# A DRAM intermediate laid out by partition of a unit instead of by lines of eight columns

## The chip, the cores and the metric

The kernel runs on one core of one Trainium2 chip. The metric is the device time of one execution in microseconds (us). A measurement of a kernel is the median of several executions. Beside it stands one execution that the hardware profiler recorded; from it come the views of the profile.

## The reference: what is computed

The input x has 32 images of 48 channels, 64 rows and 128 columns, all float32. Two layers of the same form follow one another. Each normalises x in 16 groups of channels (per image), sends the result through four recurrent scans, and adds the outcome to x. A step of a scan is a 5-tap convolution over the line before it, plus a bias, plus the line's own input:

```python
def step(w, b):
    def f(carry, inp):
        nxt = inp + _conv1d(carry, w, b)
        return (nxt, nxt)
    return f
...
x = x + _L0_conv_ref(_gn(x), ...)   # rows down, rows up, columns right, columns left
x = x + _L1_conv_ref(_gn(x), ...)   # the same with layer 1's weights
```

Down and up go over the 64 rows (the convolution runs along the columns). Right and left go over the 128 columns (the convolution runs along the rows). No line can begin before the one before it is done.

## The kernel before

**Tiling.** The 32 images are four groups of eight (`GB = 8`). Eight columns (in the row scans) or eight rows (in the column scans), each with 48 channels, make 384 values, which fill three tiles of 128 partitions (`NG = 3`, the index `o`). The table `PIECES` says which partitions hold which channels of which of the eight. A step of a scan is nine matrix products into PSUM and three vector operations (line 929) that add bias and input and write the new line in place.

**Stages.** `PHASES` is worked off in order: for layer 0 the rows of groups 0 to 3 (down and up), then the columns of the pairs (0, 1) and (2, 3) (right and left); then the same for layer 1. The profile names the products of a stage by layer and group or pair: `step_10d` is layer 1, group 0, rows down, `step_10u` the same up, `step_01l` layer 0, pair 1, columns left. In layer 1 the stages of groups 2 and 3 are joined (`JOINED`): while one group goes up, the next goes down in the same products. These steps bear two names, `step_12u7d...` for row 7 up of group 2 beside row 56 down of group 3.

**The intermediate.** The result of layer 0 goes to four DRAM tensors `mid`, one for each group of images. It is written unit by unit. A unit is one tile `o` of one group of images over a quarter of the columns: 128 partitions with 8 KB each, 1 MB in all. `keep_result` (line 852) writes it, and `by_unit` (line 269) says where it lies. Layer 1 reads it twice:

- `take_rows` (line 766) loads rows for the row scans. For these a run of DRAM bytes is short: one row, one quarter of the columns, one channel of one of the eight columns, 128 bytes for 8 images and 4 values. `by_quarter` (line 263) gives the pattern. One call takes rows `h0` to `h1` of one tile `o`, and issues a DMA for each piece of `PIECES` and each of the four quarters. Over the three tiles that is 10 pieces times 4 quarters, 40 DMAs.
- `load_residual` (line 832) loads a unit for the addition after the column scans of layer 1, with DMAs that ScalarE's queue issues.

After `take_rows` has landed, `scale_rows` (line 783, instructions on line 790) normalises the rows in place on ScalarE, 24 activations a call, eight for each `o`. Then the scan may use the rows.

**The order of the work.** Everything beside the scans is put on an agenda by the unit of scan at which it should happen, and recorded between the scan's steps. On each engine, and on each queue, the instructions of the agenda stay in that order. Nearly all DMAs are issued by one queue, SyncE's (line 298). For layer 1, `plan_rows` asks for 16 rows at a time in the stages of groups 0 and 1, and for 8 rows at a time in the joined stages of groups 2 and 3:

```python
if k in JOINED:
    for i in range(H // E8):
        h, t = i * E8, t0 + 2 * i * E8
        for o in range(NG):
            at(t - 34 + 2 * o, take_rows, k, h, h + E8, o)
        at(t - 17, scale_rows, k, h, h + E8)
elif k:
    for i in range(4):
        if PHASES[k][1]:
            for o in range(NG):
                t = t0 + ahead[i] - 2 + 3 * o
                at(t, take_rows, k, i * LOAD, (i + 1) * LOAD, o)
```

Between the loads the same queue writes the rows that come out of the up scans (`upa`, `upb`), and, around the beginning of layer 1, loads residuals for layer 0 (`xin`) and writes the last units of `mid`.

Of the kernel before, what the change touches and what calls it, by code (L numbers as in the profile page):

```python
# [29 lines left out]
F32 = mybir.dt.float32  # L30
# [3 lines left out]
C = 48  # L34
# [8 lines left out]
E8 = 8  # L43
FULL = 128
NG = E8 * C // FULL
NQ = 4
# [75 lines left out]
def kernel(  # L122
# [8 lines left out]
    nc = tc.nc  # L131
    B, _, H, W = x.shape
    NK = W // E8
    NH = H // E8
# [4 lines left out]
    LINE = E8 * RUN  # L139
# [15 lines left out]
    dram = ctx.enter_context(tc.tile_pool(name="dram", bufs=1, space=bass.MemoryType.DRAM))  # L155
# [35 lines left out]
    def kept(name):  # L191
# [11 lines left out]
            for g in range(NGRP)  # L203
        ],
        [
            dram.tile([NQ, NH, E8 * C, LINE], F32, tag=f"mid{g}", name=f"mid{g}")
            for g in range(NGRP)
        ],
    ]
# [35 lines left out]
    def x_by_col(t, e, j):  # L245


        return t[e * NQ + j]
# [10 lines left out]
    def natural_col(t, e, j):  # L259

        return t.rearrange("c (a i) q n -> i q c a n", i=E8)[e, j]

    def by_quarter(t, e, h0, h1, q):


        t = t[q].rearrange("a (i c) (e n) -> e c (a i) n", i=E8, e=E8)
        return t[e, :, h0:h1]

    def by_unit(t, o, j):


        at = [(o * FULL, 0, FULL)]
        if o == NG - 1:
            at = [(6 * C, 0, 2 * C), (5 * C + C // 3, 2 * C, FULL)]
        t = t[j].rearrange("a m n -> m a n")
        return [(t[r : r + p1 - p0], p0, p1) for r, p0, p1 in at]

    def by_line(t):

        return t.rearrange("p (a n) -> p a n", a=NH)  # L280
# [16 lines left out]
    def dma(dst, src, queue=None):  # L297
        (queue or nc.sync).dma_start(dst, src)
# [21 lines left out]
    def pieces(o):  # L320
        return [(e, c0, c1, p0) for e, c0, c1, g, p0 in PIECES if g == o]
# [3 lines left out]
    def slots(k):  # L325

        return (0, 1, 2) if k % 2 == 0 else (2, 1, 0)
# [398 lines left out]
    def place(k, h):  # L726


        first = k
        while first in JOINED:  # L730
            first -= 1
        since = k - first
        turned = (since + 1) // 2 % 2 if h < HALF else since % 2
        c = h % HALF // E8
        return HALF // E8 - 1 - c if turned else c

    def rows_at(k, h0, h1):

        places = sorted(place(k, h) for h in range(h0, h1, E8))
        at = places[0] * E8 + h0 % E8  # L740
        assert h0 // HALF == (h1 - 1) // HALF and places[-1] - places[0] == len(places) - 1
        return row_views(k)[h0 // HALF][:, :, at : at + h1 - h0]
# [23 lines left out]
    def take_rows(k, h0, h1, o):  # L766

        _, layer, g = PHASES[k]
        turned = h1 - h0 > E8 and place(k, h0) > place(k, h0 + E8)
        if turned:  # L770
            for h in range(h0, h1, E8):
                take_rows(k, h, h + E8, o)
            return
        view = rows_at(k, h0, h1)
        for e, c0, c1, p0 in pieces(o):
            here = view[p0 : p0 + c1 - c0, o]
            for q in range(NQ):
                dma(
                    here[:, :, q * RUN : (q + 1) * RUN],
                    by_quarter(source[layer][g], e, h0, h1, q)[c0:c1],  # L780
                )
# [24 lines left out]
    def quarter(k, j):  # L806
        return slot[slots(k)[j % 3]].rearrange("p (o s n) -> p s o n", s=2, o=NG)
# [24 lines left out]
    def load_residual(k, j, i, nat):  # L832
        _, layer, pair = PHASES[k]
        o, half = UNITS[i]
        t = source[layer][2 * pair + half]
        if layer:
            for there, p0, p1 in by_unit(t, o, j):
                dma(by_line(nat)[p0:p1], there, nc.scalar)
        else:
            for e, c0, c1, p0 in pieces(o):  # L840
                here = nat[p0 : p0 + c1 - c0]
                if pair or half:
                    dma(here, x_by_col(t, e, j)[c0:c1])
                else:
                    dma(by_line(here), natural_col(t, e, j)[c0:c1])
# [6 lines left out]
    def keep_result(k, j, i):  # L852
        _, layer, pair = PHASES[k]
        o, half = UNITS[i]
        for there, p0, p1 in by_unit(source[1][2 * pair + half], o, j):
            dma(there, by_line(quarter(k, j)[:, half, o])[p0:p1])

    def by_image(t):

# [210 lines left out]
    def plan_rows(k, t0, prev):  # L1070
# [11 lines left out]
# [12 lines that stand above are left out]
                else:  # L1094
                    at(t0 + ahead[i], move_rows, k, i * LOAD, (i + 1) * LOAD, False)
                at(t0 + scaled[i], scale_rows, k, i * LOAD, (i + 1) * LOAD)
# [19 lines left out]
    def plan_cols(k, t0, prev):  # L1116
# [32 lines left out]
        for u, (t, j, i) in enumerate(direct):  # L1149
            nat = tiles[u % n]  # L1150
            o, half = UNITS[i]
            if u < n:
                at(left + 16, load_residual, k, j, i, nat)
            if layer == 0:
                if u >= n:
                    at(max(direct[u - n][0] + 3, t - 21), load_residual, k, j, i, nat)
                at(t, add_residual, k, j, i, nat)
                at(t + 4, keep_result, k, j, i)
                unit = quarter(k, j)[:, half, o]
                if half == 0:  # L1160
                    for b in range(GB):
                        at(t + 5 + b, stats[0].take, j, o, unit, b)
                else:
                    at(t + 1, stats[1].take, j, o, unit)
            else:

                at(t, add_residual, k, j, i, nat)
                at(t + 2.5, permute_unit, k, j, i, nat, (nc.gpsimd, nc.scalar, nc.scalar))
                if final or j not in HELD:
                    at(t + 4.5, store_result, k, j, i, nat)  # L1170
                else:
                    at(t + 4.5, hold_result, j, i, nat)
                if final and j == 1:
                    at(t + 4.7, load_residual, k, 0, i, last_tiles(k)[i])

                if u >= 2 and u - 2 + n < len(direct):
                    at(t + 4.6, load_residual, k, *direct[u - 2 + n][1:], tiles[(u - 2) % n])
# [27 lines left out]
    for k, (kind, *_) in enumerate(PHASES):  # L1205
        n = (H if kind == "rows" else W) - 1
# [283 lines left out]
```

## Time and profile before

| what | us |
|---|---|
| median of 3 runs | 4110.29 (4107.43 to 4110.69) |
| profiled execution, its own time | 4108.49 |
| its span, first to last instruction | 4106.8 |
| TensorE (PE) busy | 4012.3 |
| VectorE (DVE) busy | 2078.8 |
| ScalarE (ACT) busy | 1306.9 |
| GpSimd (POOL) busy | 789.0 |

The span is what the profile shows; 1.7 us of the execution lie outside it. Mean granted clock of TensorE is 0.991 of full speed. SyncE (SP) only issues DMAs, so it has no busy time in this table; its issues stand in the timeline under SPq, as start, duration, what is written and read, and how many. ScalarE's queue stands under ACTq.

### The profile page before, as it was taken

The numbers are of one execution on the slowest core, as the hardware profiler recorded it, in microseconds if no ns is written. First come the engines' busy times: TensorE is split into PE (matmuls) and PEld (weight loads), VectorE is DVE, ScalarE is ACT, GpSimd is POOL, SyncE is SP. The second block draws the span as 40 slices with busy tenths as digits, with TensorE's granted clock in tenths as the row PEclk, the third lists the DMA queues.
The fourth block names the chain that finished last, engine by engine and source line by source line (L and its number), as shares of the span: only waits on it lengthen the run. The fifth ranks groups of instructions, "written<-read, shape, count | busy, mean of one in ns | idle before, by whom it ended". The sixth has DMA issues, their size and how long they took to land. (4 is left out here: it accounts for less than half of the span.)

```text
span 4106.8 us, 85201 instructions
## 1 busy us (share of the span) xinstructions
PE 4012.3 (98%) x34360; PEld 3927.0 (96%) x34360; DVE 2078.8 (51%) x6137; ACT 1306.9 (32%) x2628; POOL 789.0 (19%) x672
## 2 busy tenths in 40 slices
PE   6999999999999999999999999999999999999994
PEld 5999999999999999999999998888999999999994
DVE  6454454544444567546655443333444444444444
ACT  4557466430000355003773633434000002300122
POOL 5631303100000243002411000000000025610353
PEclk9999999999999999999999999999999999999997
DMA  9898897967993499804996965666698039999799
GB/s 299 220 223 185 245 189 218 171 108 97 147 181 60 141 245 288 193 2 155 242 161 143 142 102 96 101 108 104 103 166 202 1 77 245 299 251 155 147 234 196
DMA packets 2253898, 681.57 MB, mean 166 GB/s; under 512 B 2008848, under 2 KB 2206656, under 8 KB 2231232
## 3 DMA queue, kind: packets, MB, share of 16 engines
q1 hardware_dynamic: 2117568, 595.36, 70.3%
q10 hardware_dynamic: 135936, 80.77, 8.2%
q8 instruction: 270, 4.42, 0.5%
q14 instruction: 124, 1.02, 0.1%
HBM read 399.11 MB, written 295.93 MB: 169 GB/s over the span
## 5 line engine op out<-in xcount | busy, mean ns | idle before, releaser
L850 POOL TENSOR_TENSOR arena<-arena 128x2048 f32<-128x2048 f32 x80 | 362.5, 4547 | 1714.3 <-PE step_00l L915 521.3
L790 ACT ACTIVATE arena<-arena,offsetr,scaler 128x128 f32<-128x128 f32 (+1 forms) x576 | 345.2, 688 | 348.8 <-DMA arena<-mid 322.5
L648 ACT ACTIVATE early<-arena 128x256 f32<-128x256 f32 x192 | 129.7, 676 | 837.0 <-POOL arena L850 830.6
L790 ACT ACTIVATE arena<-arena,offset,scale 128x256 f32<-128x256 f32 (+2 forms) x360 | 249.0, 787 | 91.8 <-DMA arena<-xin 81.6
L709 POOL COPY arena<-arena 128x256 f32<-128x256 f32 x340 | 201.0, 653 | 383.7 <-DMA arena<-in_x 230.2
L915 PE MATMUL step_01r<-arena,early 128*128 128x128 f32 x2286 | 249.8, 272 | 0.0
L915 PE MATMUL step_11r<-arena,early 128*128 128x128 f32 x2286 | 249.2, 272 | 0.0
L915 PEld LDWEIGHTS step_11r<-arena,early 128*128 128x128 f32 x2286 | 248.7, 184 | 0.4 <-DVE arena L929 0.3
L915 PEld LDWEIGHTS step_01r<-arena,early 128*128 128x128 f32 x2286 | 248.9, 184 | 0.2
L915 PE MATMUL step_00r<-arena,early 128*128 128x128 f32 x2286 | 248.8, 272 | 0.0
L915 PEld LDWEIGHTS step_00r<-arena,early 128*128 128x128 f32 x2286 | 248.5, 184 | 0.2 <-DVE arena L929 0.2
L915 PE MATMUL step_10l<-arena,wleft 128*128 128x128 f32 x2286 | 248.5, 272 | 0.0
L915 PE MATMUL step_11l<-arena,wleft 128*128 128x128 f32 x2286 | 248.5, 272 | 0.0
L915 PE MATMUL step_00l<-arena,wleft 128*128 128x128 f32 x2286 | 248.4, 272 | 0.0
L915 PE MATMUL step_01l<-arena,wleft 128*128 128x128 f32 x2286 | 248.4, 272 | 0.0
L915 PE MATMUL step_10r<-arena,early 128*128 128x128 f32 x2286 | 248.4, 272 | 0.0
L915 PEld LDWEIGHTS step_10l<-arena,wleft 128*128 128x128 f32 x2286 | 248.4, 184 | 0.0
L915 PEld LDWEIGHTS step_11l<-arena,wleft 128*128 128x128 f32 x2286 | 248.4, 184 | 0.0
L915 PEld LDWEIGHTS step_00l<-arena,wleft 128*128 128x128 f32 x2286 | 248.4, 184 | 0.0
L915 PEld LDWEIGHTS step_01l<-arena,wleft 128*128 128x128 f32 x2286 | 248.4, 184 | 0.0
L915 PEld LDWEIGHTS step_10r<-arena,early 128*128 128x128 f32 x2286 | 248.4, 184 | 0.0
L872 ACT COPY arena<-arena 128x256 f32<-128x256 f32 x172 | 99.6, 656 | 366.6 <-POOL arena L850 234.7
(545 smaller groups left out, 6870.1 us busy)
## 6 DMA issues: line engine op xcount, KB each, us to landing
xin<-arena SPq DMA_DIRECT2D x94, 512.0 KB, 4.5
arena<-in_x SPq DMA_DIRECT2D x18, 2048.0 KB, 10.5
upa<-arena SPq DMA_DIRECT2D x192, 192.0 KB, 3.8
arena<-upa SPq DMA_DIRECT2D x96, 384.0 KB, 9.9
arena<-xin SPq DMA_DIRECT2D x96, 384.0 KB, 10.6
upb<-arena SPq DMA_DIRECT2D x192, 192.0 KB, 3.9
arena<-upb SPq DMA_DIRECT2D x96, 384.0 KB, 10.9
arena<-xin SPq DMA_DIRECT2D x174, 192.0 KB, 4.2
```

What stands on the lines that cost most here:

```text
L648: nc.scalar.activation(junk[:, 0:n], view[:, b], AF.Identity, accum_out=self.sum[:, i, j : j + 1])
L709: copy(dst[:, r, q], src[:, r0 + r, q])
L790: nc.scalar.activation(args[0], args[0], AF.Identity, bias=args[2], scale=args[1])
L850: eng.tensor_tensor(unit, unit, nat, ALU.add)
L872: copy(by_w(perm)[:, a], src[:, a])
L915: nc.tensor.matmul(part(turn(whole(ps[o]))[0:m], -s), weights[:, i, at : at + m], part(turn(src(i)), s), start=seen[o] == 1, stop=seen[o] ...
```

## The change

The DRAM tensors `mid` change from [quarter, row block of 8, 384, 256] to [quarter, 384, 2048]. A partition of a unit, which lay in eight runs of 1 KB, now lies in one run of 8 KB. The same bytes are written and read.

For `keep_result` and `load_residual` the access becomes plain, 128 partitions by 2048 elements. For `take_rows` the row index now lies in two dimensions of DRAM, the block of eight rows and the row within it, with different strides, where it was one dimension before. So 16 rows are no longer one pattern: the function calls itself for each 8 rows. Before, it did so only for places that run backwards.

```diff
-            dram.tile([NQ, NH, E8 * C, LINE], F32, tag=f"mid{g}", name=f"mid{g}")
+            dram.tile([NQ, E8 * C, NH * LINE], F32, tag=f"mid{g}", name=f"mid{g}")
...
     def by_quarter(t, e, h0, h1, q):
-        t = t[q].rearrange("a (i c) (e n) -> e c (a i) n", i=E8, e=E8)
-        return t[e, :, h0:h1]
+        t = t[q].rearrange("(i c) (a e n) -> e a c i n", i=E8, a=NH, e=E8)
+        return t[e, h0 // E8, :, h0 % E8 : h0 % E8 + h1 - h0]
...
     def by_unit(t, o, j):
         at = [(o * FULL, 0, FULL)]
         if o == NG - 1:
             at = [(6 * C, 0, 2 * C), (5 * C + C // 3, 2 * C, FULL)]
-        t = t[j].rearrange("a m n -> m a n")
-        return [(t[r : r + p1 - p0], p0, p1) for r, p0, p1 in at]
+        return [(t[j, r : r + p1 - p0], p0, p1) for r, p0, p1 in at]
...
     def take_rows(k, h0, h1, o):
-        turned = h1 - h0 > E8 and place(k, h0) > place(k, h0 + E8)
-        if turned:
+        if h1 - h0 > E8:
             for h in range(h0, h1, E8):
                 take_rows(k, h, h + E8, o)
             return
...
-                dma(by_line(nat)[p0:p1], there, nc.scalar)
+                dma(nat[p0:p1], there, nc.scalar)
...
-            dma(there, by_line(quarter(k, j)[:, half, o])[p0:p1])
+            dma(there, quarter(k, j)[p0:p1, half, o])
```

In the instructions, the change is on two queues. The first place is SyncE's queue where it first loads rows for layer 1, behind the last units of `mid` of a column quarter (shapes are partitions, rows and elements; `mid_84` is group 0's intermediate). Before:

```order
L298 DMA mid_87<-arena 96x8x256
L298 DMA mid_87<-arena 32x8x256
L298 DMA arena<-mid_84 48x16x32 x8
L298 DMA arena<-mid_84 32x16x32 x4
L298 DMA arena<-mid_84 16x16x32 x4
L298 DMA arena<-mid_84 48x16x32 x8
L298 DMA arena<-mid_84 16x16x32 x4
L298 DMA arena<-xin_82 48x2048 x2
```

And with the change (its line numbers are one lower from here on):

```order
L297 DMA mid_87<-arena 96x2048
L297 DMA mid_87<-arena 32x2048
L297 DMA arena<-mid_84 48x8x32 x8
L297 DMA arena<-mid_84 32x8x32 x4
L297 DMA arena<-mid_84 48x8x32 x8
L297 DMA arena<-mid_84 32x8x32 x4
L297 DMA arena<-mid_84 16x8x32 x4
L297 DMA arena<-mid_84 48x8x32 x8
L297 DMA arena<-mid_84 16x8x32 x8
L297 DMA arena<-mid_84 48x8x32 x8
L297 DMA arena<-mid_84 16x8x32 x4
L297 DMA arena<-xin_82 48x2048 x2
```

The 28 loads of 16 rows have become 56 loads of 8 rows, and the load from `xin` behind them stands 28 places later on the queue.

The second place is ScalarE's queue, where it loads the first residuals of layer 1. Before:

```order
L298 DMA arena<-mid_84 128x8x256
L298 DMA arena<-mid_85 128x8x256
L298 DMA early<-mid_84 96x8x256
L298 DMA early<-mid_84 32x8x256
L872 COPY arena<-arena 128x256 x15
```

And with the change:

```order
L297 DMA arena<-mid_84 128x2048
L297 DMA arena<-mid_85 128x2048
L297 DMA early<-mid_84 96x2048
L297 DMA early<-mid_84 32x2048
L870 COPY arena<-arena 128x256 x15
```

Their number and order stay; only the shape is another. TensorE, VectorE and GpSimd have the same instructions in the same order in both kernels.

## Prediction, on record before the result

> **What bounds the kernel now.** I read first the busy times, then the span in three stretches, then who issues the loads, then how early they land.
>
> ```profile
> PE 4012.3 (98%) x34360; PEld 3927.0 (96%) x34360; DVE 2078.8 (51%) x6137; ACT 1306.9 (32%) x2628; POOL 789.0 (19%) x672
> ...
> 82.30:4050.30 3968.00, 3964.95 (x34139) 3891.95 (x34137) 1999.81 (x6014) 1252.83 (x2526) 731.21 (x566) 1.00 0.78 162
> 4050.30:4106.80 56.50, 0.00 (x0) 0.00 (x0) 24.82 (x19) 13.31 (x23) 12.73 (x18) 0.51 1.30 170
> ```
>
> The second and third rows are stretches of the span (length, then PE, PEld, DVE, ACT and POOL busy, clock, DMA share, GB/s). From 82 to 4050 us PE is busy 3964.95 of 3968.00 us: the chain of scan steps runs without a pause. Then come 56.5 us of final stores. The edit touches no step, so between 82 and 4050 it can gain next to nothing; it can lose, if rows come late. Whether they do is decided on SyncE's queue, here where layer 1 begins (start, duration, what, how many):
>
> ```profile
> 1998.71 22.81 SPq L298 DMA_DIRECT2D arena<-mid  x28
> ...
> 2023.52 12.87 SPq L298 DMA_DIRECT2D arena<-mid  x12
> ...
> 2039.35 16.31 SPq L298 DMA_DIRECT2D arena<-mid  x12
> ...
> 2056.29 18.83 SPq L298 DMA_DIRECT2D arena<-mid  x28
> ...
> 2080.42 18.69 SPq L298 DMA_DIRECT2D arena<-mid  x28
> ...
> 2101.37 10.21 SPq L298 DMA_DIRECT2D arena<-mid  x12
> ...
> 2114.11 10.09 SPq L298 DMA_DIRECT2D arena<-mid  x12
> ...
> 2126.22 21.29 SPq L298 DMA_DIRECT2D arena<-mid  x28
> ...
> 2212.65 50.96 SPq L298 DMA_DIRECT2D arena<-mid  x80
> 2263.71 39.70 SPq L298 DMA_DIRECT2D upb<-arena  x40
> 2303.50 50.79 SPq L298 DMA_DIRECT2D arena<-mid  x80
> 2354.39 19.89 SPq L298 DMA_DIRECT2D upb<-arena  x20
> ```
>
> Group 0's 160 loads take 131.10 us together (the first eight rows), group 1's 101.75 (two rows). 2212.65 + 50.96 + 39.70 + 50.79 ends at 2354.3, where the next row begins: the queue has no free time. It goes on so through the joined stages:
>
> ```profile
> 2505.00 8.99 SPq L298 DMA_DIRECT2D upb<-arena  x10
> 2514.04 21.34 SPq L298 DMA_DIRECT2D arena<-mid  x40
> 2535.52 9.03 SPq L298 DMA_DIRECT2D upb<-arena  x10
> 2544.59 15.42 SPq L298 DMA_DIRECT2D arena<-mid  x28
> ...
> L915 PE MATMUL step_12u15d<-arena,early x18: 366/379/379, 2869.9 to 2873.5; 128*128 128x256 f32 x12, 128*96 128x240 f32 x4, 128*112 128x256 f32 x2
> L915 PE MATMUL step_12u7d<-arena,early x18: 366/379/379, 2900.5 to 2904.2; 128*128 128x256 f32 x12, 128*96 128x240 f32 x4, 128*112 128x256 f32 x2
> ```
>
> One round of 40 loads and 10 writes goes from 2514.04 to 2544.59, 30.55 us, and the eight double steps that use it take 2900.5 − 2869.9 = 30.6 us. So queue and PE are level there: a delay that the queue has when the joined stages begin is still there at their end. What is to spare shows between the end of the scaling (ACT) and the first product that needs the rows:
>
> ```profile
> ACT arena L790 <- DMA arena<-mid: 322.5, 49, 21.2
> ...
> 2149.28 6.06 ACT L790 ACTIVATE arena<-arena,offsetr,scaler 128x256 f32<-128x256 f32 x8 [0.54 <-DMA arena<-mid]
> 2870.81 4.18 ACT L790 ACTIVATE arena<-arena,offsetr,scaler 128x128 f32<-128x128 f32 x8 [3.27 <-DMA arena<-mid]
> ...
> L915 PE MATMUL step_10d<-arena,early x1134: 266/275/377, 2070.3 to 2195.7; 128*128 128x128 f32 x126, 128*96 128x120 f32 x63
> ```
>
> The scaling waits for the loads 49 times: it ends when they let it. Group 0's last 16 rows are scaled at 2149.28 + 6.06 = 2155.3. The 63 steps from 2070.3 to about 2196 take 1.99 us each at most, so row 48 is begun some 47 steps after 2070.3, at 2163: 8 us to spare. The last rows of the joined stages are ready at 2870.81 + 4.18 = 2875.0 and needed at 2900.5: 25.5 us to spare.
>
> **The change part by part.** *More issues.* Groups 0 and 1 had 320 loads of 16 rows; they become 640 of 8 rows. The joined stages already use 8 rows, so the price of the new form stands in the profile: 21.34 us for 40, 0.534 us each. A group now takes 320 × 0.534 = 170.7 us of the queue.
>
> - Group 1: 170.7 − 101.75 = **+69.0 us**.
> - Group 0: 170.7 − 131.10 = **+39.6 us** at least. Its present loads are slower than group 1's by 131.10 − 101.75 = 29.35 us, since they stand between large transfers. If all of that stays, it is +69.0 us. Smaller DMAs leave the transfer engines more room to clear the large ones meanwhile, but the queue still has to wait where a large one fills it; I take the middle, **+54.3**.
>
> Together +123.3 us, with bounds of 108.6 and 138.0. The room that I speak of stands in this stretch of the joined loads (DMA share before the last number):
>
> ```profile
> 2514.00:2535.40 21.40, 21.40 (x102) 18.36 (x101) 7.62 (x17) 8.37 (x16) 0.00 (x0) 1.00 0.54 85
> ```
>
> The 16 engines are used for 0.54 of it, so the queue's issuing, not the data, sets the 0.534 us. The Trainium skill, "DMA: Bandwidth & Descriptors", section "Rules for kernel authors", says to join small transfers, since below 64 KB a transfer is mostly overhead; the change splits 96 KB into 48 KB, and the share of 0.54 agrees.
>
> *What hides it.* PE can wait only once for a delay of the queue: by the end of the joined stages it has lost the largest excess of delay over what was to spare. The delay is the full 123.3 from the end of group 1's loads on, and the least to spare after that is 25.5. So PE stands 123.3 − 25.5 = **97.8 us** later (83.1 to 112.5). The first part falls in group 0's down scan: 54.3 − 8 = 46 us by row 48. Behind these loads on the queue stand `xin` loads, `upb` writes and the joined loads; they shift with it, and what shifts no more than PE costs nothing more.
>
> *Clock.* After a pause PE starts slower:
>
> ```profile
> 76.50 7.72 PE L915 MATMUL step_00d<-arena,early 128*128 128x128 f32 x43 [4.07 <-DVE arena L929]
> 80.00:120.00 40.00, 39.25 (x348) 39.05 (x346) 18.18 (x57) 15.99 (x36) 24.51 (x16) 0.97 0.79 125
> ```
>
> 43 products took 7.72 us where 348 later ones took 39.25 (4.85 for 43): 2.9 us lost after a pause of 4.07. Between two late loads this only shortens the next wait, because the queue sets the time; only the last pause counts, 0 to 3 us, taken as **+2**.
>
> *8-KB runs.* The new form of unit transfers stands in the profile as `spill`, same size, runs of 8 KB:
>
> ```profile
> mid<-arena SPq DMA_DIRECT2D x32, 1024.0 KB, 12.5
> arena<-mid ACTq DMA_DIRECT2D x29, 1024.0 KB, 10.9
> spill<-arena SPq DMA_DIRECT2D x24, 1024.0 KB, 12.8
> arena<-spill SPq DMA_DIRECT2D x24, 1024.0 KB, 10.3
> ...
> 4054.07 6.75 ACTq L298 DMA_DIRECT2D arena<-mid  x2
> ```
>
> 12.8 against 12.5 us to landing for the write, 10.3 against 10.9 for the read: **0**, hidden under PE until 4050. In the final stores ScalarE's queue spends 6.75 us on its last two residual loads before it copies on; with fewer, longer runs at most these go: bounds −7 and 0. I take 0, since the stores behind keep the DMA share at 1.30 there (second row of the stretches).
>
> Sum: 4108.5 (the profiled execution's own time) + 97.8 + 2 = **4208.3**. That execution is 1.8 us below the median of the runs, less than their spread of 3.3, so I predict **4208**; its own range is 4108.5 + 83.1 to 4108.5 + 112.5 + 3, that is 4192 to 4224.
>
> **Rivals.**
>
> *Cheaper issues.* The median of all row loads' own durations is lower than 0.534:
>
> ```profile
> L298 SPq DMA_DIRECT2D arena<-mid x960: 302/470/5160, 1998.7 to 2867.5; - x192
> ```
>
> At 0.470 us 640 issues take 300.8, against 232.85 now: +68.0, less 25.5, 4151. For it: the DMA engines are half free. Against it: the pitch of 40 in a row, which includes what lies between two issues, was 0.534.
>
> *Hidden.* The loads run so far ahead that nothing comes late: 4108. It needs the extra issues to cost under 25.5 us in all, 0.08 us each, and under 8 us by group 0's last rows; no row is near that. The same page of the Trainium skill, section "Issuing engines are not separate DMA queues", calls the time to issue a DMA usually small beside the DMA itself, which is this rival; 0.534 us at a share of 0.54 disagrees.
>
> *Faster.* If the queue kept up and the final loads gained all 6.75 us: 4102. For it only the ACTq row above.
>
> *Pitch.* All channels of a row block now lie 8 KB apart. If this doubled the transfer time of short runs, the share of 0.54 would become 1.08, and 40 loads would take 21.34 × 1.08 = 23.0 us, 1.7 more; over the 32 blocks of 8 rows in four groups +54, so 4262. The Trainium skill, same page, section "Latency and other measured facts", reports slower copies at row pitches of 512 KiB and more in powers of two; no run here shows such a pitch. Against it: layer 0's rows come from `xin`, which has this 8-KB pitch.
>
> ```profile
> 531.56 44.43 SPq L298 DMA_DIRECT2D arena<-xin  x40
> ```
>
> These 40 loads bring 32 rows, which take 50.96 us for 80 loads from `mid`.
>
> **How the numbers follow.** Forecast 0.65, cheaper issues 0.15, pitch 0.07, hidden 0.07, faster 0.06. A change under 0.2% (8 us) can't be told from none. Faster: 0.06. Same: 0.07. Slower: 0.65 + 0.15 + 0.07 = 0.87. The range of 4150 to 4240 holds the forecast's own range with some miss on both sides, and the cheaper issues; it leaves out pitch, hidden and faster, 0.20.
>
> **What would show it.** The down scan of group 0 (`step_10d`), 125 us now, should last some 170, with PE waiting for VectorE and that for ACT line 790. SyncE's 8-row loads of group 1 should show about 21.3 us for 40. `step_12u7d` should begin near 2998 instead of 2900.5, and from there to the end the times should be the same, 1206 us. It is wrong if `step_10d` keeps its length, if PE's waits come from a residual load, or if 40 loads take far from 21 us.

## The result and the profile after

The changed kernel takes **4210.38 us** (median of four runs, 4204.76 to 4212.57); the kernel before took 4110.49 us beside it (four runs, 4107.43 to 4116.85). The ratio is **1.0239**, with a 95% interval of 1.0221 to 1.0257: slower by 2.4%. The forecast was 4208 us. The profiled execution took 4212.57 us, with a span of 4210.8 us.

The page's busy times, and the two stretches of the span that answer to those of before (length; PE, PEld, DVE, ACT and POOL busy; clock; DMA share; GB/s):

```profile
PE 4025.9 (96%) x34360; PEld 3939.6 (94%) x34360; DVE 2078.1 (49%) x6137; ACT 1307.0 (31%) x2628; POOL 788.8 (19%) x672
...
82.30:4154.00 4071.70, 3977.57 (x34124) 3903.40 (x34124) 1997.35 (x6009) 1252.92 (x2526) 731.12 (x566) 0.99 0.76 158
4154.00:4210.80 56.80, 1.14 (x11) 0.95 (x9) 25.71 (x21) 13.35 (x23) 12.71 (x18) 0.55 1.29 173
```

The final stores are as long as before (56.80 against 56.5 us). All of the loss lies in the first stretch, which is 103.7 us longer, although PE is busy there only 12.6 us longer: PE waits where it had not waited. PE's waits, with the sum, the count and the longest, show where:

```profile
PE step_11d L913 <- DVE arena L927: 23.1, 2, 13.8
...
PE step_10d L913 <- DMA arena<-mid: 18.2, 1, 18.2
PE step_10d L913 <- DVE arena L927: 18.1, 1, 18.1
PE step_11u62d L913 <- ACT arena L788: 15.5, 1, 15.5
PE step_10d L913 <- DMA mid<-arena: 14.3, 1, 14.3
```

Before, PE waited 0.2 us in `step_10d` and nothing that the view lists in the other two. The waits stand in the down scans of group 0 (`step_10d`) and group 1 (`step_11d`) and in the first joined step (`step_11u62d`), 89.2 us together; no wait of over 1 us stands later. Whether a row names VectorE, ScalarE or a DMA, the cause is one: the rows come late. Each of the three waits in `step_10d` ends 0.5 us after a scaling of its rows has ended, those that are put down to a DMA too (start, duration; in brackets how long the engine had stood idle, and what the profile names as the end of that):

```profile
2166.71 5.98 ACT L788 ACTIVATE arena<-arena,offsetr,scaler 128x256 f32<-128x256 f32 x8 [10.27 <-DMA arena<-mid]
...
2173.18 33.66 PE L913 MATMUL step_10d<-arena,early 128*128 128x128 f32 x288 [18.23 <-DMA arena<-mid]
```

The scaling ends at 2166.71 + 5.98 = 2172.69, PE goes on at 2173.18; the other two pairs are 2120.15 and 2120.64, 2224.41 and 2224.89. And the scalings wait for SyncE's queue (start, duration, what, how many):

```profile
2003.23 34.75 SPq L297 DMA_DIRECT2D arena<-mid  x56
...
2039.98 17.87 SPq L297 DMA_DIRECT2D arena<-mid  x24
...
2060.32 20.28 SPq L297 DMA_DIRECT2D arena<-mid  x24
...
2081.19 31.40 SPq L297 DMA_DIRECT2D arena<-mid  x56
...
2117.40 31.67 SPq L297 DMA_DIRECT2D arena<-mid  x56
...
2150.58 14.46 SPq L297 DMA_DIRECT2D arena<-mid  x24
...
2166.55 15.16 SPq L297 DMA_DIRECT2D arena<-mid  x24
...
2183.69 33.12 SPq L297 DMA_DIRECT2D arena<-mid  x56
...
2279.29 89.76 SPq L297 DMA_DIRECT2D arena<-mid  x160
2369.15 39.57 SPq L297 DMA_DIRECT2D upb<-arena  x40
2408.82 86.78 SPq L297 DMA_DIRECT2D arena<-mid  x160
```

These are the same row groups as before, each with twice the number of loads. Group 0's eight add up to 198.71 us (131.10 before, **+67.6**), group 1's two to 176.54 us (101.75 before, **+74.8**): 142.4 us more of the queue. Group 1's loads end at 2408.82 + 86.78 = 2495.6, where they ended at 2354.3: 141.3 us later.

How busy the 16 DMA engines are during such a load (the last number but one) says what this time is made of. Before:

```profile
2212.60:2263.60 51.00, 51.00 (x466) 50.70 (x466) 27.87 (x107) 0.00 (x0) 2.06 (x6) 1.00 0.84 142
```

After:

```profile
2279.00:2369.00 90.00, 90.00 (x821) 89.39 (x820) 45.19 (x156) 30.06 (x41) 3.77 (x12) 1.00 0.49 82
```

0.84 of 51.0 us is 42.8 us, 0.49 of 90.0 is 44.1: the data need the engines for about the same time in both. What has grown is the time to issue twice as many DMAs, and in it the engines stand half idle.

PE pays not for the 142.4 us but for what is left after the spare time. Before, the rows that the first joined step needs, and the step itself:

```profile
2409.92 4.18 ACT L790 ACTIVATE arena<-arena,offsetr,scaler 128x128 f32<-128x128 f32 x8 [3.54 <-PE step_11d L915]
...
2448.38 4.01 PE L915 MATMUL step_11u62d<-arena,early 128*128 128x256 f32 x18
```

They were scaled by 2409.92 + 4.18 = 2414.1 and used from 2448.4 on: 34.3 us to spare. After, with the last scaling of the joined stages and the step that needs it:

```profile
2547.87 4.15 ACT L788 ACTIVATE arena<-arena,offsetr,scaler 128x128 f32<-128x128 f32 x8 [2.45 <-DMA arena<-mid]
...
2552.07 5.52 PE L913 MATMUL step_11u62d<-arena,early 128*128 128x256 f32 x16 [15.46 <-ACT arena L788]
...
2996.55 4.19 ACT L788 ACTIVATE arena<-arena,offsetr,scaler 128x128 f32<-128x128 f32 x8 [1.77 <-PE step_12u10d L913]
...
L913 PE MATMUL step_10d<-arena,early x1134: 266/275/553, 2073.9 to 2255.8; 128*128 128x128 f32 x126, 128*96 128x120 f32 x63
...
L913 PE MATMUL step_12u7d<-arena,early x18: 366/379/379, 3005.7 to 3009.3; 128*128 128x256 f32 x12, 128*96 128x240 f32 x4, 128*112 128x256 f32 x2
```

The rows are scaled at 2552.0, 137.9 us later than before, and PE starts on them at once: 137.9 − 34.3 = **103.6 us** late. (A step's nine products are eighteen instructions in the trace; the first two of this step had gone ahead at 2536.0, so the row shows sixteen.) From there on the delay stays: `step_12u7d` begins at 3005.7 instead of 2900.5 (+105.2), with its rows ready at 2996.55 + 4.19 = 3000.7, 5.0 us ahead. From there to the end it takes 1205.1 us, before 1206.3.

### The profile page after: what moved, and what is told of

It is laid out like the page before. It is cut to its first block, busy times and chain, and to the rows that moved or that the text cites. A ratio compares the mean times of both kernels' runs of the same rounds, so it can differ in the third digit from the quotient of the medians.

```text
span 4210.8 us, 85576 instructions
## 1 busy us (share of the span) xinstructions
PE 4025.9 (96%) x34360; PEld 3939.6 (94%) x34360; DVE 2078.1 (49%) x6137; ACT 1307.0 (31%) x2628; POOL 788.8 (19%) x672
## 5 line engine op out<-in xcount | busy, mean ns | idle before, releaser
L647 ACT ACTIVATE early<-arena 128x256 f32<-128x256 f32 x192 | 129.6, 675 | 846.5 <-POOL arena L848 818.9
```

What stands on the lines that cost most here:

```text
L647: nc.scalar.activation(junk[:, 0:n], view[:, b], AF.Identity, accum_out=self.sum[:, i, j : j + 1])
```

## The experiments

The kernel before took 4109.52 us beside the first four (seven runs, 4107.22 to 4112.87), 4106.98 us beside the fifth and sixth (4105.75 to 4109.07) and 4107.39 us beside the last (4105.2 to 4108.96). The theory is that twice as many issues on SyncE's queue make the rows late; its chief rival is that the new layout makes them late.

**The split without the layout (e1).** The kernel before, with the old layout, but every group of 16 rows loaded as two groups of 8:

```diff
-        turned = h1 - h0 > E8 and place(k, h0) > place(k, h0 + E8)
-        if turned:
+        if h1 - h0 > E8:
```

> The kernel before with its 1-KB runs, but every row load split to 8 rows: the doubled issues alone, without the new layout. Theory of the issues (the queue's 320 additional DMAs set the loss): as slow as the change, 4210 us, within some 8 us; group 1's loads take about 88 us for 160 and group 0's about 199 us in all. Rival, the layout (8 KB between neighbouring channels, or the longer runs, slow the loads): 4110 us, as before.

Measured: 4217.93 us (4213.52 to 4221.36), ratio 1.0263, interval 1.0247 to 1.0278. The last of PE's waits stands where it stands in the changed kernel:

```profile
PE step_11u62d L914 <- ACT arena L789: 15.2, 1, 15.2
```

Group 1's loads take 89.37 and 86.48 us for 160, group 0's 200.1 us in all, as expected. The loss is there without the new layout. Whether the layout brings something by itself is not settled: the median lies 7.6 us above that of the changed kernel, but the intervals of the two ratios overlap. Of the 7.5 us between the two profiled spans, 3.8 are there at `step_12u7d` (3009.5 against 3005.7) and most of the rest comes after PE's last product. In this run and in e2 the profile puts the third wait in `step_10d`, 18.0 us, down to a load from `xin`, a residual load, which was to be a sign that the prediction is wrong; but there too PE goes on 0.5 us after the scaling of its rows (2228.70 after 2228.21, 2224.28 after 2223.79).

**The split in one group alone (e2, e3).** The same edit for group 0, and for group 1:

```diff
+        if h1 - h0 > E8 and g == 0:    # e2
+        if h1 - h0 > E8 and g == 1:    # e3
```

> Old layout, only group 0's loads split to 8 rows. Theory of the issues: the queue is late by 67.6 us (group 0's excess with the change) when group 0's last rows are loaded, 8 us are to spare there, so PE is 60 us late; what is to spare later is more, so nothing is added: 4110 + 60 = 4170 us. The theory that the prediction used, the least to spare at the end of the joined stages (25.5 us) decides, would give 4110 + 42 = 4152 us if nothing were lost earlier, but the 8 us come first, so here it gives 4170 us too. Rival, the layout: 4110 us.

> Old layout, only group 1's loads split to 8 rows. Theory of the issues: the queue is 74.8 us late at the end of group 1's loads. If the first rows of the joined stages decide (34 us to spare), PE is 40 us late, 4150 us; if the last rows of the joined stages decide with 25.5 us to spare and nothing is regained on the way, 49 us late, 4159 us. Rival, the layout: 4110 us.

Measured: 4167.09 us for group 0 (4165.49 to 4169.2; 1.014, 1.0125 to 1.0155) and 4148.01 us for group 1 (4145.58 to 4151.01; 1.0091, 1.0074 to 1.0108), 57.6 and 38.5 us slower. Group 1's loads on SyncE's queue, and PE's waits, when only group 1 is split:

```profile
2214.08 90.50 SPq L298 DMA_DIRECT2D arena<-mid  x160
...
2345.85 85.04 SPq L298 DMA_DIRECT2D arena<-mid  x160
```

```profile
PE step_11u62d L914 <- ACT arena L789: 18.1, 1, 18.1
PE step_11d L914 <- DVE arena L928: 16.2, 2, 8.2
```

90.50 + 85.04 − 101.75 = 73.8 us more of the queue, less the 34.3 us to spare at the first joined step, is 39.5; measured were 38.5. With the 25.5 us at the end of the joined stages it would have been 48. So the place that decides is the first joined step. With group 0 alone split all the new waits stand in `step_10d`, which lasts 183.3 us there; before, it lasted 125.4. 57.6 + 38.5 = 96.1 us are to be set beside e1, which has both splits in the same layout and loses 4217.93 − 4109.52 = 108.4. That is 12.3 us more than the sum: each split alone uses up spare time of its own before it costs anything, some 11 us in group 0 and 34.3 us at the first joined step, while with both the queue reaches the first joined step with the two delays added and only the 34.3 us are taken off.

**A layout with fewer loads (e4).** The intermediate laid out as `xin` is, so that one DMA brings eight rows of all four quarters, with the same 8-KB runs and the same 8-KB pitch; groups 0 and 1 then need 40 loads for what takes 80 before and 160 in the changed kernel. The transfers of units have to be cut at the pieces, since a unit isn't contiguous over its partitions any more. Against the changed kernel:

```diff
-            dram.tile([NQ, E8 * C, NH * LINE], F32, tag=f"mid{g}", name=f"mid{g}")
+            dram.tile([E8 * NQ, C, UNIT], F32, tag=f"mid{g}", name=f"mid{g}")
...
-            here = view[p0 : p0 + c1 - c0, o]
-            for q in range(NQ):
-                dma(
-                    here[:, :, q * RUN : (q + 1) * RUN],
-                    by_quarter(source[layer][g], e, h0, h1, q)[c0:c1],
-                )
+            here = view[p0 : p0 + c1 - c0, o].rearrange("p h (q n) -> p (h q) n", q=NQ)
+            dma(here, x_by_row(source[layer][g], e, h0, h1)[c0:c1])
...
-            for there, p0, p1 in by_unit(t, o, j):
-                dma(nat[p0:p1], there, nc.scalar)
+            for e, c0, c1, p0 in pieces(o):
+                dma(nat[p0 : p0 + c1 - c0], x_by_col(t, e, j)[c0:c1], nc.scalar)
...
-        for there, p0, p1 in by_unit(source[1][2 * pair + half], o, j):
-            dma(there, quarter(k, j)[p0:p1, half, o])
+        t = source[1][2 * pair + half]
+        for e, c0, c1, p0 in pieces(o):
+            dma(x_by_col(t, e, j)[c0:c1], quarter(k, j)[p0 : p0 + c1 - c0, half, o])
```

> The new 8-KB runs, but the quarters laid inside the row index (row within eight, quarter, channel, 2048), as layer 0's input has them, so that one DMA loads 8 rows of all four quarters: 320 row loads in all where the change has 1280, at the same 8 KB between channels; unit transfers are split by pieces, 160 on each queue where there were 64. Theory of the issues: 32 rows take about 44 us, as in layer 0, no rows come late, and the time is that of before, 4110 us, within 6 us. Rival, the layout: 4210 us, since the 8 KB pitch is the same as with the change.

Measured: 4390.34 us (4387.51 to 4393.16), ratio 1.0683, 1.0667 to 1.0699. Both theories missed. Groups 0 and 1 come in time (`step_10d` lasts 124.4 us), but the joined stages lose some 245 us: `step_12u7d` begins at 3149.0. There SyncE's queue waits for PE, and longer still for VectorE (185.7 us in ten waits), and PE waits for SyncE's loads:

```profile
SPq L297 <- PE step_11u62d L910: 42.6, 1, 42.6
...
SPq L297 <- PE step_11u40d L910: 28.3, 1, 28.3
```

```profile
PE step_11u22d L910 <- DMA arena<-mid: 10.8, 1, 10.8
```

This kernel changed two things at once, the loads of groups 0 and 1 and those of the joined stages; so the next one separates them.

**The same with the joined loads by quarters (e5).** In the joined stages each load is issued once per quarter again, as in the kernel before; everything else is as in e4 (its loads for the other groups stand behind these lines):

```diff
+            if k in JOINED:
+                t = source[layer][g]
+                t = t.rearrange("(i q) c (a e n) -> q e a c i n", i=E8, a=NH, e=E8)
+                for q in range(NQ):
+                    dma(here[:, :, q * RUN : (q + 1) * RUN], t[q, e, h0 // E8, c0:c1])
+                continue
```

> The layout of the run with the quarters inside the row index, with one difference: in the joined stages each row load is again issued once for each quarter (four rows of 32 values each in a piece, as before and with the change); groups 0 and 1 keep one DMA for all quarters (160 loads where the change has 640). In that run, groups 0 and 1 were as fast as before, and the joined stages lost 245 us, with SyncE waiting for TensorE and TensorE for row loads at each eight rows. If this comes from the form of the joined loads (one DMA over whole rows is held to overlap with rows that the steps still use), it goes away: 4110 us, within 8 us, and theory of the issues stands. If it comes from the layout itself (8 KB between channels, or unit transfers in pieces), it stays: over 4300 us.

Measured: 4145.24 us (4142.5 to 4149.07), ratio 1.0093, 1.0078 to 1.0108. That is neither of the two numbers, yet the rows come as the theory has it: group 1's loads on SyncE's queue, the DMA share in the first of them, and where the joined stages end:

```profile
2205.96 44.37 SPq L297 DMA_DIRECT2D arena<-mid  x40
...
2291.74 44.82 SPq L297 DMA_DIRECT2D arena<-mid  x40
...
2206.00:2250.40 44.40, 44.40 (x406) 44.10 (x405) 24.61 (x98) 0.00 (x0) 2.05 (x6) 1.00 1.00 151
...
L917 PE MATMUL step_12u7d<-arena,early x18: 366/379/380, 2897.6 to 2901.2; 128*128 128x256 f32 x12, 128*96 128x240 f32 x4, 128*112 128x256 f32 x2
```

89.2 us for what took 101.75 before and 176.5 after the change, at a DMA share of 1.00; PE reaches `step_12u7d` 2.9 us earlier than before and doesn't wait for a row of layer 1. So the 8-KB pitch shows no loss in these rows, and with few issues the engines are full. The joined loads' form was what e4 lost most by; why it makes PE and SyncE wait for each other was not followed further and stays open. The 38 us that e5 still loses come after the joined stages:

```profile
PE step_11r L917 <- DVE arena L931: 10.3, 1, 10.3
```

**The residual loads in pieces (e7).** That wait stands in the row scans, and from the start of PE's last product to the end of the span e5 takes 83.8 us, before 57.1. The suspect is ScalarE's queue, where e4 and e5 issue 160 residual loads instead of 64. The kernel before, with that alone changed:

```diff
-            for there, p0, p1 in by_unit(t, o, j):
-                dma(by_line(nat)[p0:p1], there, nc.scalar)
+            t = t[j].rearrange("a m n -> m a n")
+            for e, c0, c1, p0 in pieces(o):
+                there = t[e * C + c0 : e * C + c1]
+                dma(by_line(nat)[p0 : p0 + c1 - c0], there, nc.scalar)
```

> The kernel before, with nothing changed but the residual loads of layer 1 on ScalarE's queue: they are cut at the pieces, 160 instead of 64, as in the kernel e5_like_xin_quarters, whose rows came in time and which still took 4145 us. If these cuts are what that kernel lost: 4140 to 4150 us, PE waits some 10 us at the beginning of step_11r, the last product of layer 1's row scans comes about 9 us late, and from PE's end to the end of the span it takes about 84 us instead of 57. If the 8-KB pitch or the cut writes of layer 0's results were the cause, this kernel takes 4107 to 4112 us and none of the two marks shows.

Measured: 4144.28 us (4143.51 to 4146.8), ratio 1.0091, 1.0074 to 1.0108. Both marks show (PE's wait, then the steps of the two row scans with their first and last start):

```profile
PE step_11r L917 <- DVE arena L931: 6.5, 1, 6.5
...
L917 PE MATMUL step_11r<-arena,early x2286: 259/275/582, 3552.2 to 3810.6; 128*128 128x128 f32 x128, 128*96 128x112 f32 x63
...
L917 PE MATMUL step_11l<-arena,wleft x2286: 259/275/288, 3810.7 to 4058.8; 128*128 128x128 f32 x128, 128*96 128x112 f32 x63
```

`step_11r` ends 9.3 us later than before (3801.3), and from the last product to the end of the span, 4142.8, it takes 84.0 us. 9.3 + 26.9 = 36.2 us, of 36.0 by which the span is longer. So what e5 lost beside its own gain were the residual loads. That 96 more issues are the reason, as on SyncE's queue, is not shown. The transfers on ScalarE's queue, these loads and some stores, also took longer in all (packets, MB, their time as a share of the 16 engines' span), first before, then here:

```profile
q10 hardware_dynamic: 135936, 80.77, 8.2%
...
q10 hardware_dynamic: 137472, 80.77, 10.0%
```

8.2% of 4106.8 us are 337 us, 10.0% of 4142.8 are 414: the same bytes, 77 us more, and where these loads stand the engines are already full (a DMA share of 0.97 from 3300 us to the end before, 1.03 here). So issues and slower transfers are both left as the cause. The row loads were different: there the engines' time stayed and they stood half idle.

**More issues with hardly any data (e6).** The kernel before, with a copy of 2 KB from DRAM to DRAM behind each of the 320 row loads of groups 0 and 1; nothing reads it:

```diff
+    aside = dram.tile([320, 16, RUN], F32, tag="aside", name="aside")
...
+                if k not in JOINED:
+                    n = put_aside[0]
+                    put_aside[0] += 1
+                    dma(aside[n], x[0, 0:16, n % H, 0:RUN])
```

> The kernel before, layout and 16-row loads unchanged; behind each of the 320 row loads of groups 0 and 1 the queue issues one more DMA, of 2 KB from DRAM to DRAM, which nothing waits for. It measures an issue by itself, without splitting a load and without moving its bytes differently. Theory of the issues: an issue of that size took about 0.465 us from one to the next elsewhere, 320 of them 149 us; less the 34 us to spare at the first joined rows, 4110 + 115 = 4225 us, and not under 4190 us where the queue waits anyway. Rival (smaller loads are slow to transfer or to land, the number of issues is not the cause): 4110 to 4120 us.

Measured: 4270.25 us (4267.6 to 4272.02), ratio 1.0396, 1.0378 to 1.0413. The copies on SyncE's queue (shortest, median and longest in ns; first and last start):

```profile
L300 SPq DMA_DIRECT2D aside<-in_x x320: 494/535/3902, 2000.7 to 2551.6; - x160
```

The sign is as the theory has it and its size well beyond: PE begins `step_12u7d` at 3062.9, 162.4 us late. The price of one issue was assumed too low, 0.465 us. The rows of the first joined step show what it came to:

```profile
2604.69 4.15 ACT L796 ACTIVATE arena<-arena,offsetr,scaler 128x128 f32<-128x128 f32 x8 [2.26 <-DMA arena<-mid]
```

They are scaled at 2608.8, 194.7 us later than before, which makes 194.7 / 320 = 0.61 us for each copy, all delays included; less the 34.3 us to spare it gives 160.4 us for PE, close to the 162.4. The engines are not what holds the copies up: over the first 80 loads and copies of group 1 the DMA share is 0.43. That issues alone make the rows late, with no change of layout and next to no data, is shown.

No version beat the kernel before. e5 reached `step_12u7d` 2.9 us ahead of it, 1.1 of them already at the start of `step_10d`; whether anything would be gained if the residual loads could stay whole in its layout is not shown.

## Why the prediction was right, step by step

The total came within 2.4 us of the median, and for the reason named: more issues on SyncE's queue, late rows, and PE waiting for what is left after the spare time. That it came so close is in part luck. The queue's delay was forecast 19.1 us too small; the spare time 8.8 us too small, and 4.5 us of the delay that were regained on the way were not forecast at all, and these two take most of the first error back.

- **Group 1's loads** were forecast at +69.0 us and measured +74.8. The price was 0.534 us for a load of 8 rows, from the joined stages; here it is 176.54 / 320 = 0.552. That makes 5.8 us, all of the error of this term, and the bounds left no room for it, since that one row was taken as exact.
- **Group 0's loads** were forecast at +54.3, between 39.6 and 69.0; measured were +67.6. 5.8 us come from the same price. The rest is the choice of the middle: I took half of the 29.35 us that these loads lose between large transfers to stay, and 198.71 − 176.54 = 22.2 us stayed. The argument that smaller DMAs give the engines room for the large ones gained little. The sum of +142.4 lies beyond the upper bound of 138.0.
- **What hides it** was forecast at 25.5 us, the least spare time, at the end of the joined stages. It was 34.3 us, at their beginning. The step that failed is "the queue has no free time", and with it that a delay of the queue at the beginning of the joined stages "is still there at their end". Before, the queue had time left among the first joined loads (the last row is that of the last joined loads):

```profile
2417.37 49.39 SPq L298 DMA_DIRECT2D arena<-mid  x92
2474.24 9.13 SPq L298 DMA_DIRECT2D upb<-arena  x10
...
2853.83 14.07 SPq L298 DMA_DIRECT2D arena<-mid  x28
```

After:

```profile
2555.14 48.55 SPq L297 DMA_DIRECT2D arena<-mid  x92
2603.80 9.57 SPq L297 DMA_DIRECT2D upb<-arena  x10
...
2980.93 14.12 SPq L297 DMA_DIRECT2D arena<-mid  x28
```

  Before, 2417.37 + 49.39 = 2466.8, and the next row begins 7.5 us later, since the queue waits for VectorE (7.4 us, its longest wait in the joined stages), whose rows it is to write; after, it follows at once. The delay of the queue falls from 141.3 us at the end of group 1's loads to 137.8 at these 92, to 129.6 at the writes behind them and to 127.1 at the last joined loads; the last scaling is 125.7 us late (2996.55 against 2870.81), while PE's delay stays. So queue and PE are nearly level in the rounds that I had read, and most of what is regained is regained in one place. The delay exceeds the spare time most where it is new: at the beginning by 137.9 − 34.3 = 103.6 us, at the end by 125.7 − 25.5 = 100.2. My mistake was to set the full delay of the beginning against the spare time of the end.
- **Sum.** 137.9 − 34.3 = 103.6 us in place of 123.3 − 25.5 = 97.8.
- **Group 0's down scan.** Forecast 46 us late; `step_10d` lasts 181.9 us where it lasted 125.4, so 56.5 longer. By subtraction from the 67.6 us of the queue some 11 us were to spare, where I had 8. The length, forecast at "some 170", is 182, off by the term of group 0. PE's waits there name VectorE only once and DMAs twice, where I had expected VectorE and behind it ScalarE; that PE goes on right after the scaling holds for all three.
- **Clock.** Forecast +2. PE is 103.7 us late at the first joined step and 105.2 at `step_12u7d`, +1.5. Over the earlier pauses PE lost more (89.2 us of waits make 105.2 us with 3.6 us that PE was late before `step_10d`, so some 12 went to a lower clock; PE was busy 12.6 us longer), but between late loads that only shortens the next wait, as argued.
- **8-KB runs.** Forecast 0, in the unit transfers and in the tail (KB each, median us to landing; then ScalarE's last residual loads):

```profile
mid<-arena SPq DMA_DIRECT2D x32, 1024.0 KB, 13.3
arena<-mid ACTq DMA_DIRECT2D x29, 1024.0 KB, 10.4
...
4158.70 6.14 ACTq L297 DMA_DIRECT2D arena<-mid  x2
```

  13.3 us against 12.5, 10.4 against 10.9, 6.14 against 6.75, and a final stretch of the same length: nothing that can be told.

The rivals. *Cheaper issues* (4151) falls: the median of a row load's own duration is still 0.470 us, but what counts is the time from one issue to the next, 0.552 us. *Faster* (4102) and *hidden* (4108) fall with PE's waits. For *hidden*, the Trainium skill, "DMA: Bandwidth & Descriptors", section "Issuing engines are not separate DMA queues", calls the time to issue usually small beside the DMA itself; for these loads the trace disagrees, with 0.552 us for an issue where the load's data need the 16 engines for 44.1 / 160 = 0.28 us. *Pitch* (4262) falls by e1, which has the loss with the old pitch, and by e5, which has the 8-KB pitch and no loss in the rows.

## What to carry to other kernels

Count the issues per queue before the bytes: where a queue's own time from one DMA to the next sets the pace, cutting each DMA in two took 1.5 and 1.7 times the queue's time here (198.7 for 131.1 us, 176.5 for 101.75), and the longer runs gave nothing back that can be told. A layout is worth what it allows one DMA to bring. Price an issue from rows of the same queue in the same neighbourhood, with some per cent of error, and set a delay against the spare time at the place where the delay arises, since a queue gives back part of it further on wherever it had waited before. A second change in the same kernel (here the residual loads, which a new layout cut in pieces) has its own price, on another queue: try it alone.

## What the runs showed of the hardware that I had not expected

- The same rows need the 16 DMA engines for nearly the same time in three forms: 42.8 us as 80 loads (0.84 of 51.0), 44.1 us as 160 (0.49 of 90.0), 44.4 us as 40 (1.00 of 44.4). Only in the last are the engines full.
- A copy of 2 KB costs the queue as much as a load of mostly 48 KB: 0.535 us by itself at the median and 0.61 with all delays, against 0.470 by itself and 0.552 from one load to the next.
- 160 residual loads on ScalarE's queue instead of 64, of the same bytes, cost 36 us of the span, 26.9 of them after PE's last product, and their queue's packets took 414 us of the 16 engines instead of 337.
